# Graph layer on one core: PE results used two steps later, both sums of a two-tile batch together, fixed PSUM tiles, places turned in bfloat16

## The chip, the core and the metric

The kernel runs on one core of a Trainium2 chip. The core has TensorE (PE in the profile; PEld are its weight loads), VectorE (DVE), ScalarE (ACT), GpSimd (POOL) and SyncE (SP, which only issues DMAs here), each with an instruction stream of its own that runs in order; streams wait for each other through semaphores. The metric is the time of one execution in microseconds (us), the median of several runs.

## The reference

One layer of a graph network over 12,500 nodes of 64 features and 212,500 edges, which arrive sorted by one of their ends (`dst`), while the sums go by the other (`src`). Cut to what is computed:

```python
h = jnp.maximum(_layernorm(x, axis=-1), 0.0)
edge_in = jnp.concatenate([h[src], h[dst], edge_weight1], axis=1)
e = jax.nn.silu(edge_in @ eW1 + eb1)
e = jax.nn.silu(e @ eW2 + eb2)
agg = jax.ops.segment_sum(e, src, num_segments=h.shape[0])
node_in = jnp.concatenate([h, agg], axis=1)
out = x + jax.nn.silu(node_in @ nW1 + nb1) @ nW2 + nb2
```

## The kernel before

The nodes are dealt into NB = 100 buckets of L = 125. Two kinds of work run beside each other.

*Sending.* Edges come in 208 blocks of 1024. For each block `send` (line 439) forms the part of the first edge layer that depends on `dst` and the weight (`qp`, PE line 454), copies it to SBUF (`qs`, ACT lines 464 and 470, which also puts the place of the `src` node in its bucket beside it), and writes its rows to the table `q` in DRAM with eight indirect DMAs from POOL's queue (line 477). The row of each edge is its bucket and its rank there; `count` (line 375) finds the ranks on DVE (`oh`, `each`, `mine`, `rank`, `to`, lines 382 to 433) with PE's help (lines 396 and 414). A block is cut into three pieces.

*Steps.* The ranks are cut into twelve LEVELS; each names the tiles a batch takes (1 or 2) and the block by which its ranks are complete. A batch is one level of four buckets (G = 4), so that a level has 25 batches, and a step treats four 128-row tiles, a whole one-tile batch or half of a two-tile batch. There are 450 steps: two levels of one tile (steps 0 to 49), six of two tiles (50 to 349), four of one tile (350 to 449). Step k does, in functions of their own:

- `fetch` (519): SP loads the batch's rows `qt` from `q`, after its level's last scatter, and the buckets' `src` part `a`, unless it is kept in SBUF
- `s_lr` (560): four PE matmuls turn the places of the tiles across partitions (`lr`); `s_one_t` (569): DVE compares them with the partition number (`oneT`)
- `s_pt` (574): PE transposes the rows into `pt` and adds `a` times `oneT`; ACT takes the silu, `e1`
- `s_bias` (609): ACT writes the second bias into a PSUM tile; `s_p2` (615): PE adds `e1` times `w2` to it; ACT takes the silu, `e2`
- `s_one` (593): DVE compares places with node numbers (`one`); `s_seg` (625): PE sums `e2` by node into `seg`; `s_add` (634): DVE adds `seg` to `aggT` in SBUF

These are interleaved by hand: `manual_schedule` keeps PE, DVE, ACT and SP in program order, and `turn` says which step each function treats in turn k:

```python
turn = [
    (s_pt, 1), (s_add, -2), (s_one_t, 2), None, (s_bias, 1), (s_p2, 0), (s_one, 0), None, (s_seg, -1), None, (s_lr, 3), None,
]
```

A `None` is a place for other work: pieces of sending, spread evenly between `marks` so that a level's blocks are sent, with three blocks of lead (`LEAD`), some steps before its first; a feed of earlier stages; and, in the last level, pieces of the node layer. `nodes` (line 270) is a generator, one per batch: PE `z` from `aggT` (277), DVE adds the part of the features and ACT takes the silu (`zs`, 281 and 282), PE `o` (286), DVE adds the residual (`os`, 289). Up to two are advanced in alternate places.

PSUM has eight banks: a pool of four (`mm`) for `lr`, `pt`, `qp`, `z`, `o` and others in rotation, two for `p2`, one for `seg`, one for the counts. The fetched rows have NQ = 4 slots of two-tile size.

Of the kernel before, what the change touches and what calls it, by code (L numbers as in the profile page):

```python
# [62 lines left out]
FIRST_KEPT, LAST_KEPT = (0, 2, 5, 7, 10, 12, 15, 17, 20), 21  # L63
# [11 lines left out]
def tile_gnn(ctx: ExitStack, tc: tile.TileContext, x, src, dst, ew, eW1, eb1, eW2, eb2, nW1, nb1, nW2, nb2, out):  # L75
# [122 lines left out]
    def product(s, hr, ps, tag, to):  # L198

        abs_ = []  # L200
        for a in range(2):

            half = slice(a * D, (a + 1) * D)
            ab = ps.tile([P, G // 2, H], F32, name="ab", tag=tag)
            for i in range(G // 2):
                nc.tensor.matmul(ab[:, i], hr[half, i, :], w1[half, s, :], start=True, stop=True)  # L206
            abs_.append(ab)
        for a in range(2):
            nc.scalar.copy(to.rearrange("l (i a) h -> l a i h", a=2)[:, a], abs_[a])
# [34 lines left out]
    def node_part(B, ps, sb, tag):  # L244
# [6 lines left out]
        z = [ps.tile([P, G // 2, L], F32, name="zp", tag=tag) for _ in range(2)]  # L251
# [18 lines left out]
    def nodes(B, xr, zh, ps, sb, tag):  # L270
# [4 lines left out]
        z = [ps.tile([P, G // 2, L], F32, name="z", tag=tag) for _ in range(2)]  # L275
        for a in range(2):
            nc.tensor.matmul(z[a], w1g, aggT[:, b + a : b + G : 2, :], start=True, stop=True)
        send_out()
        yield
        for a in range(2):  # L280
            nc.vector.tensor_tensor(zs[:, a], z[a], zh[:, a], op=OP.add)
        nc.scalar.activation(zs, zs, AF.Silu, bias=nb1c)
        yield
        o = ps.tile([L, G, D], F32, name="o", tag=tag)
# [12 lines left out]
    qsp = ctx.enter_context(tc.tile_pool(name="qs", bufs=8))  # L297
    top = ctx.enter_context(tc.tile_pool(name="to", bufs=4))
    with ExitStack() as work:
        mm = work.enter_context(tc.tile_pool(name="mm", bufs=4, space=PSUM))  # L300
        p2p = work.enter_context(tc.tile_pool(name="p2", bufs=2, space=PSUM))
        sgp = work.enter_context(tc.tile_pool(name="sg", bufs=1, space=PSUM))
# [5 lines left out]
        full = sgp.tile([P, NB], F32, name="counts")  # L308
        nc.tensor.matmul(full, before, identb[:, :NB], start=True, stop=True)
        nc.vector.memset(full, -1.0)  # L310
        mine = cnt.tile([P, NB, TB], F32, name="mine")
        sums = []
# [61 lines left out]
        def count(s):  # L374

            if s < nblocks:
# [8 lines left out]
                each = wk.tile([P, NB], BF16, name="each")  # L385
# [53 lines left out]
        def send(s):  # L439
# [9 lines left out]
            qps = [mm.tile([P, 2, 2, H], F32, name="qp", tag="mm") for _ in range(2)]  # L449
# [8 lines left out]
            for i, qp in enumerate(qps):  # L458
# [7 lines left out]
            for i, same, qs in parts:  # L466
# [45 lines left out]
        steps = [(w, B, n, g) for w, B, n in batches for g in range(n)]  # L512
        PIECES = 1 + TB // G
# [3 lines left out]
        most = max(n for _, _, n in batches)  # L517

        def fetch(i):
            if i >= len(batches):  # L520
                return
            c, B, n = batches[i]
            assert not any(pending[: c + 1])
            while B not in done_a:
                next(feed)
            at = B * G * ROWS + G * (ENDS[c] - n * P)
            qt = ld2.tile([P, G * most, W], F32, name="qt")
            ins = nc.sync.dma_start(
                qt[:, : G * n, :].rearrange("p j w -> p (j w)"),
                q[at : at + G * n * P, :].rearrange("(p j) w -> p (j w)", p=P),  # L530
            ).ins
# [3 lines left out]
            tc.add_to_no_dep_group("loads", ins)  # L535
            if c == len(LEVELS) - 1 and not ndp:
# [3 lines left out]
                for name, bufs in (("nd_in", NQ + 5), ("nd", 2), ("al", NQ)):  # L540
                    ndp.append(work.enter_context(tc.tile_pool(name=name, bufs=bufs, side="right")))
            a = kept.get(B)
            if a is None:
# [4 lines left out]
                else:  # L548
                    a = ld2.tile([P, G, H], F32, name="a", bufs=NQ - 1)
                nc.sync.dma_start(a, ta_buckets[:, B * G : B * G + G])  # L550
            batch[c, B] = [qt, a, None]
            if c == len(LEVELS) - 1:
                node_in[B] = nodes_in(B, ndp[0])

        def of(k):

            c, B, n, g = steps[k]
            return batch[c, B], [((g * G + t) % n * G + (g * G + t) // n, (g * G + t) // n) for t in range(G)]

        def s_lr(k):  # L560
            (qt, _, _), tiles = of(k)
            loc = qt.rearrange("p j w -> p (j w)").bitcast(BF16)
            lr = mm.tile([P, G, P], F32, name="lr", tag="mm")
            for t, (j, _) in enumerate(tiles):
                at = 2 * (j * W + H) + 1
                nc.tensor.matmul(lr[:L, t, :], loc[:, at : at + 1].to_broadcast([P, L]), identb, start=True, stop=True)  # L566
            st[k] = {"lr": lr}

        def s_one_t(k):
            oneT = wk.tile([L, G, P], F32, name="oneT")  # L570
# [3 lines left out]
        def s_pt(k):  # L574

            (qt, a, _), tiles = of(k)
            oneT = st[k].pop("oneT")
            pt = mm.tile([P, G, P], F32, name="pt", tag="mm")
            for t, (j, _) in enumerate(tiles):
                nc.tensor.matmul(  # L580
                    pt[:, t, :], qt[:, j, :H], ident, is_transpose=True, start=t == 0, stop=False, skip_group_check=True
                )
            for b, same in itertools.groupby(range(G), lambda t: tiles[t][1]):
# [3 lines left out]
                    pt[:, cols, :], a[:L, b, :], oneT[:, cols, :], start=False, stop=True, skip_group_check=True  # L587
# [537 lines left out]
```

## Time and profile before

| | |
|---|---|
| runs | 2437.44, 2447.51, 2449.9 us; median 2447.51 |
| profiled execution | 2449.06 us, its span 2447.2 us |
| PE busy | 2047.0 us (84%), 16191 matmuls |
| DVE busy | 1882.0 us (77%) |
| POOL busy | 1723.1 us (70%), of it 1661 scatters 1691.0 us |
| ACT busy | 1101.4 us (45%) |
| granted PE clock, mean | 0.929 |

All times in the profile are from the start of the span. A line of a timeline has start, duration, engine, line of the program, operation, `out<-in` with shapes, and how many instructions of the kind were merged; in square brackets stands how long the engine had been idle before, and the instruction whose end released it. SPq and POOLq are the issuing queues. A line of waits has the engine and what waited, what it waited for, the total, the number of times and the longest one. The stretches' columns are named where they are shown.

### The profile page before, as it was taken

To read this page: it belongs to the slowest core of one execution; us is meant where nothing else is said; L and a number is where in the kernel's file an instruction comes from. 1 tells how busy PE (TensorE), PEld (TensorE's weight loads), DVE (VectorE), ACT (ScalarE), POOL (GpSimd) and SP (SyncE) were. 2 spreads that over 40 slices of the span, in tenths; PEclk is the share of its full clock that TensorE was granted. 3 is DMA by queue.
4 is the path that set the end of the run, shared out by engine and by line. 5 is a ranking of instruction groups with operands and counts; after the bars stand their busy time and mean duration, and the time that the engine had idled before them with its cause. 6 is when DMAs were issued, how large, how long until landed. Compare 5 with 4: busy or idle time off the path is not lost.

```text
span 2447.2 us, 45925 instructions
## 1 busy us (share of the span) xinstructions
PE 2047.0 (84%) x16191; PEld 1835.2 (75%) x16191; DVE 1882.0 (77%) x3058; ACT 1101.4 (45%) x2428; POOL 1723.1 (70%) x1712
## 2 busy tenths in 40 slices
PE   3673886655688898988989889999999999999998
PEld 2452665555677787877878778788888889899998
DVE  7985676666677787887878878888888888886665
ACT  2452443322344454444545444445555555555443
POOL 4677777777777777777777777777777777773210
PEclk9865898777799999999999999999999999999999
DMA  4564776555566654656644434444444444544674
GB/s 119 184 218 130 225 220 199 166 171 159 166 195 191 196 188 157 184 182 198 185 131 143 142 125 138 146 141 138 135 157 141 148 143 135 155 147 122 182 213 119
DMA packets 212956, 399.73 MB, mean 163 GB/s; under 512 B 47132, under 2 KB 112463, under 8 KB 212513
## 3 DMA queue, kind: packets, MB, share of 16 engines
q1 hardware_dynamic: 134581, 225.69, 30.8%
q0 software_dynamic: 53536, 123.03, 14.7%
q10 hardware_dynamic: 24602, 47.98, 6.8%
q8 instruction: 131, 2.15, 0.4%
q14 instruction: 106, 0.87, 0.1%
HBM read 200.58 MB, written 195.95 MB: 162 GB/s over the span
## 4 chain that ended last, share of the span: by engine, by line
PE 38%; DMA 19%; POOL 17%; DVE 14%; issue 9%; ACT 3%; SPq 0%; DVEq 0%; POOLq 0%; ACTq 0%
POOL q L477 17%; DMA q<-qs,to 16%; PE seg L632 9%; PE pt L586 8%; PE p L618 7%; PE qp L454 4%; PE pt L580 4%; PE lr L566 2%; DVE oneT L571 2%; DVE rank L431 2%; DVE each L387 1%; DVE one L599 1%; PE ab L206 1%; DVE mine L429 1%; DVE oh L382 1%
## 5 line engine op out<-in xcount | busy, mean ns | idle before, releaser
L477 POOL DMA_INDIRECT q<-qs,to x1661 | 1691.0, 1018 | 585.0 <-issue 393.2
L590 ACT ACTIVATE e<-pt 128x512 f32<-128x512 f32 x450 | 268.8, 597 | 822.3 <-PE pt L586 820.1
L632 PE MATMUL seg<-one,e 128*128 128x125 f32 x3600 | 499.1, 283 | 100.4 <-DVE aggT L643 59.3
L632 PEld LDWEIGHTS seg<-one,e 128*128 128x128 f32 x3600 | 451.5, 197 | 134.3 <-issue 74.3
L618 PEld LDWEIGHTS p<-w,e 128*128 128x128 f32 x3600 | 475.1, 197 | 46.5 <-issue 20.3
L618 PE MATMUL p<-w,e 128*128 128x128 f32 x3600 | 493.3, 281 | 0.0
L464 ACT COPY qs<-qp 128x512 f32<-128x512 f32 x416 | 224.7, 588 | 343.6 <-PE qp L454 292.5
L571 DVE TENSOR_SCALAR oneT<-lr,part 125x512 f32<-125x512 f32 x450 | 335.2, 745 | 52.5 <-PE lr L566 52.0
L431 DVE TENSOR_REDUCE rank<-mine 128x8 f32<-128x800 f32 x208 | 334.7, 1609 | 7.2
L599 DVE TENSOR_TENSOR one<-nodes,qt 128x500 f32<-128x500 f32 x450 | 301.8, 671 | 0.0
L454 PE MATMUL qp<-win,pick 64*128 64x256 f32 x1662 | 271.0, 438 | 35.2 <-DMA pick<-in_edge_weight_dram 15.2
L622 ACT ACTIVATE e<-p 128x512 f32<-128x512 f32 x450 | 269.1, 598 | 43.6 <-PE p L618 43.6
L580 PE MATMUL pt<-ident,qt 128*128 128x128 f32 x1800 | 286.7, 284 | 0.8 <-DVE oneT L571 0.8
L433 DVE SCALAR_TENSOR_TENSOR to<-rank,offE 128x8 int32<-128x8 f32 x208 | 36.5, 175 | 301.3 <-DMA q<-qs,to 296.4
L612 ACT COPY p<-b2f 128x512 f32<-128x512 f32 x450 | 267.2, 594 | 0.0
L643 DVE TENSOR_TENSOR aggT<-aggT,seg 128x500 f32<-128x500 f32 x275 | 184.1, 670 | 78.4 <-PE seg L632 78.1
L454 PEld LDWEIGHTS qp<-win,pick 64*128 64x128 f32 x1662 | 168.5, 206 | 101.1 <-issue 61.4
L586 PE MATMUL pt<-oneT,al 125*128 125x256 f32 (+1 forms) x1048 | 228.8, 351 | 13.4 <-DVE oneT L571 13.4
L580 PEld LDWEIGHTS pt<-ident,qt 128*128 128x128 f32 x1800 | 199.4, 147 | 43.7 <-issue 36.6
L429 DVE TENSOR_TENSOR mine<-oh,counts 128x800 f32<-128x800 bf16 x208 | 204.0, 981 | 19.2 <-PE counts L414 18.2
L387 DVE TENSOR_REDUCE each<-oh 128x100 bf16<-128x800 bf16 x208 | 205.1, 986 | 7.1
L566 PE MATMUL lr<-identb,qt 128*125 128x128 bf16 x1800 | 182.5, 225 | 24.3 <-DMA qt<-q 13.7
(156 smaller groups left out, 1847.0 us busy)
## 6 DMA issues: line engine op xcount, KB each, us to landing
qt<-q SPq DMA_DIRECT2D x150, 576.0 KB
qt<-q SPq DMA_DIRECT2D x150, 288.0 KB
q<-zeros ACTq DMA_DIRECT2D x25, 1080.0 KB
q<-qs,to POOLq DMA_INDIRECT x1661
q<-zeros ACTq DMA_DIRECT2D x10, 1440.0 KB
bc<-dests SPq DMA_DIRECT2D x103, 128.0 KB
win<-tb SPq DMA_DIRECT2D x416, 30.0 KB
a<-ta SPq DMA_DIRECT2D x45, 256.0 KB
```

The lines of the kernel that those rows point to most:

```text
L431: nc.vector.tensor_reduce(rank, mine.rearrange("p b t -> p t b"), AX.X, OP.add)
L454: nc.tensor.matmul(qps[i][:, t, : n_of[t]], pick[at, t * P : (t + 1) * P], win[at, : n_of[t]], start=True, stop=True)
L477: ins = nc.gpsimd.indirect_dma_start(out=q[:], out_offset=bass.IndirectOffsetOnAxis(ap=to[:k, j : j + 1], axis=0), in_=qs[:k, t, a, :], in ...
L571: nc.vector.tensor_scalar(oneT, st[k].pop("lr")[:L], part1[:L, :], None, op0=OP.is_equal)
L580: nc.tensor.matmul(pt[:, t, :], qt[:, j, :H], ident, is_transpose=True, start=t == 0, stop=False, skip_group_check=True)
L586: nc.tensor.matmul(pt[:, cols, :], a[:L, b, :], oneT[:, cols, :], start=False, stop=True, skip_group_check=True)
L590: nc.scalar.activation(e1, pt, AF.Silu)
L599: nc.vector.tensor_tensor(one.rearrange("p (b j) l -> p b j l", j=n), nodes1[:, None, None, :].to_broadcast(wide), loc[:, tiles[0][1] : ti ...
L612: nc.scalar.copy(p2, b2f)
L618: nc.tensor.matmul(p2[:, t, :], e1[:, t, :], w2, start=False, stop=t == G - 1, skip_group_check=True)
L622: nc.scalar.activation(e2, p2, AF.Silu)
L632: nc.tensor.matmul(item[2][:, b, :], e2[:, t, :], one[:, t, :], start=j < G, stop=j >= G * (n - 1))
```

## The change

- `turn` becomes one in which pt runs two steps ahead of p2 and seg two behind it (before: one and one); the load of a batch is issued six steps ahead, in slots for single steps (eight half slots), and `a` is loaded by a function of its own, four steps ahead; three `None` in place of four.
- `s_seg` treats both steps of a two-tile batch at the second of them.
- DVE's order in a turn becomes one, oneT, add (before: add, oneT, one); ACT's becomes e1, e2, bias (before: e1, bias, e2), with the bias written into the tile that e2 of two steps before has read.
- PSUM: eight tiles that live throughout, four of them handed out in rotation by `bank`; both halves of `z` share the bank of the counts, and one DVE addition takes them.
- `nodes` are advanced by `tick` at each `None`: z, zs, o and os of a batch at successive places, the next batch's z where the last one's os stands.
- `lr` is made by transposes with a bfloat16 result instead of matmuls with a float32 result.
- Fewer buckets' `a` are kept in SBUF: of the first pass 2, 8 and 15 (before: nine), then all up to 16 (before: 21).
- Halves are copied in reversed order in `product` and `send`; `each` has two fixed tiles; several pools get other numbers of buffers (`e1` 3, `one` and `e2` 4, from 2).

The core of the diff:

```diff
-FIRST_KEPT, LAST_KEPT = (0, 2, 5, 7, 10, 12, 15, 17, 20), 21
+FIRST_KEPT, LAST_KEPT = (2, 8, 15), 16
...
         zs = sb.tile([P, 2, G // 2, L], F32, name="zs", bufs=3)
-        z = [ps.tile([P, G // 2, L], F32, name="z", tag=tag) for _ in range(2)]
+        z = z_of()
         for a in range(2):
-            nc.tensor.matmul(z[a], w1g, aggT[:, b + a : b + G : 2, :], start=True, stop=True)
+            nc.tensor.matmul(z[:, a], w1g, aggT[:, b + a : b + G : 2, :], start=True, stop=True)
         send_out()
         yield
-        for a in range(2):
-            nc.vector.tensor_tensor(zs[:, a], z[a], zh[:, a], op=OP.add)
+        nc.vector.tensor_tensor(zs, z, zh, op=OP.add)
         nc.scalar.activation(zs, zs, AF.Silu, bias=nb1c)
         yield
-        o = ps.tile([L, G, D], F32, name="o", tag=tag)
+        o = o_of()
...
-        mm = work.enter_context(tc.tile_pool(name="mm", bufs=4, space=PSUM))
-        p2p = work.enter_context(tc.tile_pool(name="p2", bufs=2, space=PSUM))
-        sgp = work.enter_context(tc.tile_pool(name="sg", bufs=1, space=PSUM))
+        psum = work.enter_context(tc.tile_pool(name="psum", bufs=1, space=PSUM))
+        p2s = [psum.tile([P, G, H], F32, name=f"p2{i}") for i in range(2)]
+        seg = psum.tile([P, 4 * P], F32, name="seg")[:, : G * L].rearrange("p (b l) -> p b l", l=L)
+        free = itertools.cycle([psum.tile([P, 4 * P], F32, name=f"bank{i}") for i in range(4)])
...
-        def fetch(i):
-            if i >= len(batches):
+        def fetch(k):
+            if k in batch or k not in first_of:
                 return
...
+            i = k % (2 * NQ)
+            qt = qts[i // 2][:, i % 2 * G : (i % 2 + n) * G, :]
...
+            tc.declare_no_dep(ins, group="turned", reason="the comparison that read the places came after them")
...
+        def s_a(k):
+            c, B, n, g = steps[k]
+            if g == 0:
+                rows[c, B] = rows_of_a(c, B)
...
-            lr = mm.tile([P, G, P], F32, name="lr", tag="mm")
-            for t, (j, _) in enumerate(tiles):
-                at = 2 * (j * W + H) + 1
-                nc.tensor.matmul(lr[:L, t, :], loc[:, at : at + 1].to_broadcast([P, L]), identb, start=True, stop=True)
+            lr = bank(1, 2 * P)[:, 0].bitcast(BF16).rearrange("p (u e) -> p u e", u=G)
+            for u, (j, _) in enumerate(tiles):
+                loc = qt[:, j, H : H + 1].bitcast(BF16)[:, 1:2]
+                ins = nc.tensor.transpose(lr[:L, u, :], loc.to_broadcast([P, L]), identb).ins
...
-            p2 = p2p.tile([P, G, H], F32, name="p2")
-            nc.scalar.copy(p2, b2f)
-            st[k]["p2"] = p2
+            nc.scalar.copy(p2s[k % 2], b2f)
...
-            e2, one = st[k].pop("e2"), st[k].pop("one")
-            for t, (j, b) in enumerate(tiles):
-                nc.tensor.matmul(item[2][:, b, :], e2[:, t, :], one[:, t, :], start=j < G, stop=j >= G * (n - 1))
+            for i in range(k - n + 1, k + 1) if g == n - 1 else ():
+                e2, one = st[i].pop("e2"), st[i].pop("one")
+                for u, (j, b) in enumerate(of(i)[2]):
+                    nc.tensor.matmul(seg[:, b, :], e2[:, u, :], one[:, u, :], start=j < G, stop=j >= G * (n - 1))
...
+        def tick():
+
+            for t in list(going):
+                t[1] += 1
+                if next(t[0], 0) == 0:
+                    going.remove(t)
+            if tails and all(i > 2 for _, i in going):
+                B = tails.pop(0)
+                going.append([nodes(B, *node_in.pop(B), lambda: zb, lambda: bank(1, G, D)[:L, 0], ndp[1]), 1])
+                next(going[-1][0])
...
         turn = [
-            (s_pt, 1), (s_add, -2), (s_one_t, 2), None, (s_bias, 1), (s_p2, 0), (s_one, 0), None, (s_seg, -1), None, (s_lr, 3), None,
+            (s_pt, 2), (s_a, 4), (s_one, -1), (fetch, 6), (s_one_t, 3), (s_add, -3), None,
+            (s_p2, 0), (s_bias, 2), None, (s_seg, -2), None, (s_lr, 4),
         ]
...
-        first = -3
+        first = -4
...
-            start = w * (NB // G) - NQ
-            by = sum(x[2] for x in batches[: start + 1]) - 2
+            by = sum(n for _, _, n in batches[: w * (NB // G)]) - 6.5
...
-                    if tails:
-                        both = tails[at % 2 :: 2][:1] if len(tails) > 1 else tails[:1] * (at % 2)
-                        for t in both:
-                            if next(t, 0) == 0:
-                                tails.remove(t)
+                    tick()
```

More of the change, by code (lines that the diff above doesn't have):

```diff
@@ L250, in node_part @@
             yield
[L251 removed]
+        z = [bank(G // 2, L) for _ in range(2)]
         for a in range(2):
@@ L311, in tile_gnn @@
         mine = cnt.tile([P, NB, TB], F32, name="mine")
+        eachs = [cnt.tile([P, NB], BF16, name=f"each{i}") for i in range(2)]
         sums = []
```

154 lines of the change are left out of this document (79 added, 75 removed).

## The prediction

> **What bounds the kernel now.** I read the page first, then busy time by stretch, cut where one level of steps gives way to the next: steps 300-349 (two tiles a batch), then 350-374, 375-399, 400-424 and 425-449 (one tile a batch).
>
> ```profile
> span 2447.2 us, 45925 instructions
> ...
> 100.00:1835.00 1735.00, 1420.00 (x10792) 1248.11 (x10793) 1330.74 (x2125) 767.74 (x1736) 1334.17 (x1317) 0.91 0.54 170
> 1835.00:2030.00 195.00, 189.56 (x1569) 173.35 (x1568) 167.56 (x263) 104.05 (x223) 150.02 (x148) 1.00 0.45 143
> 2030.00:2128.00 98.00, 93.93 (x866) 88.67 (x866) 88.00 (x142) 50.20 (x106) 75.37 (x75) 1.00 0.50 149
> 2128.00:2222.00 94.00, 91.46 (x854) 87.97 (x854) 80.14 (x129) 48.78 (x102) 67.51 (x66) 1.00 0.50 149
> 2222.00:2310.00 88.00, 87.96 (x831) 86.30 (x830) 57.36 (x95) 43.84 (x87) 23.26 (x24) 1.00 0.46 133
> 2310.00:2447.00 137.00, 126.33 (x1080) 122.86 (x1078) 77.78 (x152) 56.05 (x98) 18.78 (x23) 0.99 0.60 175
> ```
>
> Columns: stretch, length, busy us and count of PE, PE loads, DVE, ACT and POOL, granted clock, DMA share, GB/s. POOL looks a quarter idle, but its own timeline says otherwise.
>
> ```profile
> 38.85 1.05 POOL L477 DMA_INDIRECT q<-qs,to  x1 [21.34 <-ACT qs L470]
> ...
> 2199.75 0.97 POOL L477 DMA_INDIRECT q<-qs,to  x1 [0.30 <-issue]
> 2201.03 0.97 POOL L477 DMA_INDIRECT q<-qs,to  x1 [0.30 <-issue]
> ...
> 2227.22 1.13 POOL L477 DMA_INDIRECT q<-qs,to  x1 [11.91 <-ACT qs L470]
> ...
> 2292.66 0.90 POOL L477 DMA_INDIRECT q<-qs,to  x1 [2.82 <-ACT qs L470]
> ```
>
> Each scatter holds POOL for 0.97 + 0.30 = 1.27 us, a block of eight for 10.2; in 100-1835, 1317 of them fill 1735 us. There POOL sets the pace, and what PE gains or loses is worth nothing. Beside steps 300-349 run 19 blocks (194 us of POOL in 195): balance. Beside 350-374 run ten (102 in 98), then eight, then three: POOL drops out (it first goes hungry before 2227), and PE is busy for 96-100%. From about 1835 on PE, with what it waits for, is the bound. Those waits of PE, nine rows from first to last, sum to 15.7 us:
>
> ```profile
> PE lr L566 <- DMA qt<-q: 4.8, 5, 1.1
> ...
> PE counts L414 <- DVE u L407: 0.4, 1, 0.4
> ```
>
> The last 25 steps also carry the node layer. One turn of that stretch, with the ACT and DVE work that matters:
>
> ```profile
> 2412.41 0.36 PEld L566 LDWEIGHTS <-qt 128*125 128x125 bf16 x4
> 2412.52 0.39 PE L566 MATMUL lr<-identb,qt 128*125 128x128 bf16 x4
> 2412.69 0.42 PEld L580 LDWEIGHTS pt<-ident,qt 128*128 128x128 f32 x4
> 2412.72 0.68 DVE L643 TENSOR_TENSOR aggT<-aggT,seg 128x500 f32<-128x500 f32 x1 [0.47 <-PE seg L632]
> 2413.09 0.97 PEld L586 LDWEIGHTS pt<-oneT,a_last 125*128 125x128 f32 x8
> 2413.32 0.74 DVE L571 TENSOR_SCALAR oneT<-lr,part 125x512 f32<-125x512 f32 x1
> 2413.98 0.73 PEld L277 LDWEIGHTS z<-aggT,w1g 128*128 128x128 f32 x4
> 2414.73 1.07 PEld L618 LDWEIGHTS p<-w,e 128*128 128x128 f32 x8
> 2414.78 0.59 ACT L612 COPY p<-b2f 128x512 f32<-128x512 f32 x1
> 2415.72 0.95 PEld L286 LDWEIGHTS o<-w2n,zs 128*125 128x125 f32 x8
> 2416.03 0.60 ACT L622 ACTIVATE e<-p 128x512 f32<-128x512 f32 x1 [0.65 <-PE p L618]
> 2416.52 0.70 ACT L282 ACTIVATE zs<-zs,nb1c 128x500 f32<-128x500 f32 x1
> 2416.59 0.97 PEld L632 LDWEIGHTS seg<-one,e 128*128 128x128 f32 x8
> 2417.48 0.36 PEld L566 LDWEIGHTS <-qt 128*125 128x125 bf16 x4
> ```
>
> A turn is 2417.48 - 2412.41 = 5.07 us, and PE never stops. It can do so because `o` at 2415.72 uses the `zs` of the turn before: this turn's is begun only at 2416.52.
>
> **The last stretch after the change.** The changed program's streams have, per turn: PE transposes, pt, z, p2, seg, o, lr; ACT e1, e2, bias, zs; DVE one, oneT, add, os, zs. Three things move: `add`, which `z` needs, comes behind `oneT`; `o` waits for the `zs` of its own turn; and the bias copy refills the PSUM tile that `e2` has just read, so it waits for `e2`, with `zs` queued behind both. What a handover costs is seen where PE stood still at the end:
>
> ```profile
> 2435.94 0.68 DVE L643 TENSOR_TENSOR aggT<-aggT,seg 128x500 f32<-128x500 f32 x1 [0.46 <-PE seg L632]
> 2436.67 0.72 PEld L277 LDWEIGHTS z<-aggT,w1g 128*128 128x128 f32 x4 [0.96 <-DVE aggT L643]
> ...
> 2438.34 0.71 ACT L282 ACTIVATE zs<-zs,nb1c 128x500 f32<-128x500 f32 x1 [3.00 <-DVE zs L281]
> 2439.10 0.95 PEld L286 LDWEIGHTS o<-w2n,zs 128*125 128x125 f32 x8 [0.63 <-ACT zs L282]
> 2440.28 0.42 DVE L289 TENSOR_TENSOR os<-o,xr 125x256 f32<-125x256 f32 x1 [1.16 <-PE o L286]
> ```
>
> 0.05 us each (2436.62 to 2436.67, 2439.05 to 2439.10). The new turn, counted from the issue of lr:
> - lr ends at 2412.52 + 0.39, so 0.50 after its issue; handover 0.05; oneT and add 0.74 + 0.68, less 0.08 overlap (add to oneT started 0.60 apart, add lasting 0.68), 1.34; handover 0.05. So z at 1.94, where PE alone would be there at 1.57: 0.37 lost.
> - z to p2 0.75 (2413.98 to 2414.73). p2's issue to e2 1.30 (to 2416.03). e2 0.60 + 0.05, then bias; zs 0.49 behind bias, as now behind e2; zs 0.70; handover 0.05: o comes 3.19 after p2. PE's own work between is p2 0.99 (to 2415.72) and seg 0.89 (2416.59 to 2417.48), 1.88: 1.31 lost.
> - o 0.87 (2415.72 to 2416.59). Sum 1.94 + 0.75 + 3.19 + 0.87 = 6.75 us, 1.68 more than now.
>
> Every link hangs on the one before it, round to the next lr, so nothing hides it. From the lr of step 430 to that of step 449 the present kernel makes 19 turns of 5.07, 96.3 us. The changed one starts z a turn later: one turn without (about 3.35) and 18 of 6.75, 124.9: +28.6. From there to the end it takes 2440.70 - 2417.48 = 23.2 us now. Changed: two more turns with bias (6.75, and 6.1 without lr), two without bias (0.75 + 1.30 + 0.49 + 0.70 + 0.05 + 0.87 = 4.2 each), three of z, seg and o at about 3.5 (z 1.1, DVE 0.7, ACT 0.7, o 0.9 and handovers), 0.7 for the last o and os: 32.3, +9.1. Together +37.7. If bias did not wait, 18 x 0.16 = 3 less; were each of the five handovers twice as dear, 5 more.
>
> **Steps 350-424.** There add falls due once a turn too:
>
> ```profile
> 2132.09 1.05 PE L632 MATMUL seg<-one,e 128*128 128x125 f32 x8
> 2134.44 0.67 DVE L643 TENSOR_TENSOR aggT<-aggT,seg 128x500 f32<-128x500 f32 x1
> 2135.02 0.74 DVE L571 TENSOR_SCALAR oneT<-lr,part 125x512 f32<-125x512 f32 x1
> 2135.44 1.05 PE L632 MATMUL seg<-one,e 128*128 128x125 f32 x8
> ```
>
> A turn is 3.35 us. Seg ended at 2133.14, DVE was busy with a block's ranks, add began 1.30 late and ended at 2135.11, just before the next seg. With oneT ahead of it (0.66) it ends at 2135.77, and seg waits some 0.4 us; queued behind seg are lr and so the next oneT. DVE is busy for 88 of 98 us here, so this recurs about once a block: 21 blocks x 0.4 = +8. Bounds: 0 (the qp group between two segs gives cover) and 0.5 in each of 50 turns, 25. For two-tile batches add has a turn more to spare, and both sums together cost PE what they cost apart: 0.
>
> **Smaller terms.** PE's 15.7 us of waits: the load now comes two turns ahead of lr instead of one, e1 and e2 two turns ahead of their use; I take -8, bounds 0 and -15.7. The other way, at step 350 the first load follows its level's last scatters two turns ahead of lr where it was four.
>
> ```profile
> SPq L528 <- DVE one L599: 1260.3, 274, 12.3
> ...
> SPq L528 <- DMA q<-qs,to: 19.0, 4, 12.3
> ...
> L391 DVE TENSOR_SCALAR pick<-bc,same,plus 128x512 f32<-128x512 bf16 x102 | 55.8, 547 | 0.0
> ```
>
> SP's queue stands 1260 us behind `one` today, with the edge weights' and windows' loads behind it; the load now takes a slot whose `one` is a turn old, so that wait goes, and since those loads cost PE next to nothing (the rows of its waits), so does the gain. SP has waited for scatters up to 12.3 us; two turns less of cover is 7.8; I take +3 (0 to 8), since three blocks are still sent ahead. Earlier levels: 0, under POOL. The places as bf16 transposes: same operands and count, so 0 for PE; at most what the float32 transposes take (0.40 against 0.28 a group, rows above) x 125 turns, +15. For oneT I keep 0.74: its output and its source memory stay; at best it gets as short as the 547 ns of `pick`, -0.2 x 18 = -4. (The Trainium skill, VectorE: DVE Perf Modes, "What auto-detection actually checks", asks 16 bits of every tensor for two elements a cycle out of PSUM; oneT writes float32, so by it the sum stays as it is.) Rows of `a` are loaded 104 times instead of 45 because fewer stay in SBUF; they come two turns ahead of pt, twice the lead that left `qt` 4.8 us of waits, so 0; without that cover, up to 1.1 us each for the 24 that fall into steps 350-424. Fixed slots in SBUF and PSUM and copies in reversed order issue nothing more: 0. Three places a turn for the scattered pieces instead of four: the same pieces, 0 under POOL, and in 350-424 the reason why I don't count on more cover for add than now.
>
> **Sum.** 2447.2 + 37.7 + 8 + 3 - 8 = 2487.9 us of span; outside it lie 2449.06 - 2447.2 = 1.9, and the profiled run is 1.6 above the median of 2447.51. So 2488, 1.7% slower.
>
> **Rivals.**
> - Faster, 2432: the two steps of slack do what they say, all 15.7 us of waits go, and the last turns stay at 5.07. Place: `o`, in the turn of its own zs. It decides at 1.88 us: if zs is there that soon after p2, PE does not stop. For: e2 to zs is 0.49 today. Against: e2 itself begins only 1.30 after p2, so 1.88 leaves no room for the bias copy and zs.
> - Only z's 0.37 is lost, o being covered by something I don't see: 2447.5 + 18 x 0.37 + 3 + 3 = 2460.
> - No change, 2447: POOL paces on to the end. Against: its 11.91 us of hunger before 2227, with PE at 100%.
> - Worse, 2525: add is late in every turn of 350-424 (25), the boundary costs 8, and transposes go at the float32 pace (15).
> - The clock: PE's granted share falls as lr becomes a transpose. Rows: 1.00 in 2222-2310, with four transposes among 831 / 25 = 33 matmuls a step; 0.91 in 100-1835, where PE waits on POOL. At 0.91 the 612 us from 1835 would last 60 longer: 2508 without the rest, 2548 with it. The Trainium skill (TensorE: Matmul & The Clock Gate, "Part 4: PE-mode transpose") says that transposes don't count as busy for the clock gate, which speaks for this rival; the 1.00 beside transposes speaks against it.
>
> **Chances and range.** Forecast 0.72 (its own range 2466 to 2512), faster 0.08, only z 0.08, no change 0.03, worse 0.07, clock 0.02. The range 2456 to 2512 takes in "only z" and leaves out both signs beyond. About 0.5% (12 us) is what a measurement can tell from no change: faster 0.08, same 0.06 (no change and part of "only z"), slower 0.86.
>
> **What would show it.** Right: in the changed profile PE idles before `o` for about 1.3 us, released by ACT zs, and before `z` for 0.4, released by DVE add, some 20 times each; turns of 6.7 us; PE busy falls well below 100% in the last 150 us. POOL's last scatter stays within 10 us of 2293. Wrong: turns near 5.1 with PE full, or the loss lying before the last scatter, or a granted clock under 0.98 in the end.

## The result and the profile after

The changed kernel takes 2480.88 us (median of four runs, 2478.09 to 2486.47) where the kernel before takes 2446.66 beside it: a ratio of 1.0149, with a 95% interval of 1.0116 to 1.0182. Predicted were 2488 us. The profiled execution spans 2478.8 us.

The same stretches as before, from the view of busy time by stretch of the changed kernel (stretch, length, busy us and count of PE, PE loads, DVE, ACT, POOL, then granted clock, DMA share, GB/s), and the end of POOL's timeline:

```profile
2030.00:2128.00 98.00, 89.03 (x789) 83.24 (x790) 84.07 (x137) 50.69 (x100) 75.15 (x76) 0.98 0.51 157
2128.00:2222.00 94.00, 90.34 (x832) 85.62 (x831) 75.88 (x124) 50.94 (x98) 62.65 (x61) 1.00 0.50 155
2222.00:2310.00 88.00, 86.19 (x812) 84.62 (x811) 55.27 (x90) 46.94 (x84) 19.25 (x19) 1.00 0.46 141
2310.00:2479.00 169.00, 135.17 (x1071) 123.96 (x1069) 74.11 (x128) 58.40 (x96) 18.76 (x25) 0.98 0.47 137
```

```profile
2289.73 0.90 POOL L485 DMA_INDIRECT q<-qs,to  x1 [6.02 <-ACT qs L478]
```

PE, which was busy for 92 to 100% of the stretches from 2030 on, is now busy for 91% of the first of them (96 before) and 80% of the last (92 before). POOL's last scatter comes at 2289.73 (2292.66 before), so POOL is not the reason. The granted clock is 0.98 in the first and the last of these stretches (1.00 and 0.99 before); 0.02 of 98 and of 169 us is 5 us at most (an estimate), and in the turns from 2320 to 2450 it is 1.00, so the clock is not the reason either. The three waits from 1835 on that the prediction turns on, before (line, releaser: us in total, times, longest):

```profile
PE z L277 <- DVE aggT L643: 2.4, 3, 0.9
PE seg L632 <- DVE aggT L643: 2.4, 3, 1.2
PE o L286 <- ACT zs L282: 0.5, 1, 0.5
```

After, the three longest of PE:

```profile
PE bank L284 <- ACT zs L280: 25.0, 25, 1.6
PE seg L647 <- DVE aggT L657: 12.5, 19, 2.6
PE bank L604 <- DVE oneT L588: 6.8, 6, 2.5
```

L284 is `o`: each of the 25 node layers makes PE stand for 1 us. The wait of `z` is not among them, since the modelled ends of the matmuls leave some 0.1 us of it; it shows in the weight loads, which come first (from 2311 on; `counts` is the bank in which `z` now lies):

```profile
PEld bank L284 <- ACT zs L280: 29.9, 25, 2.0
PEld counts L276 <- DVE aggT L657: 5.4, 19, 0.3
```

One turn of the last stretch, PE's weight loads (PEld) beside DVE and ACT:

```profile
2433.24 0.31 PEld L582 LDWEIGHTS <-qt 128*125 128x125 bf16 x4
...
2433.73 0.75 DVE L588 TENSOR_SCALAR oneT<-bank,part 125x512 f32<-125x512 bf16 x1 [2.89 <-PE bank L582]
...
2434.40 0.67 DVE L657 TENSOR_TENSOR aggT<-aggT,seg 128x500 f32<-128x500 f32 x1
...
2435.11 0.72 PEld L276 LDWEIGHTS counts<-aggT,w1g 128*128 128x128 f32 x4 [0.28 <-DVE aggT L657]
...
2435.86 1.07 PEld L635 LDWEIGHTS p<-w,e 128*128 128x128 f32 x8
...
2437.16 0.60 ACT L639 ACTIVATE e<-p 128x512 f32<-128x512 f32 x1 [1.50 <-PE p L635]
2437.79 0.59 ACT L630 COPY p<-b2f 128x512 f32<-128x512 f32 x1
2438.31 0.71 ACT L280 ACTIVATE zs<-zs,nb1c 128x500 f32<-128x500 f32 x1
...
2439.07 0.95 PEld L284 LDWEIGHTS bank<-w2n,zs 128*125 128x125 f32 x8 [1.25 <-ACT zs L280]
2439.94 0.31 PEld L582 LDWEIGHTS <-qt 128*125 128x125 bf16 x4
```

The turn is 2439.94 - 2433.24 = 6.70 us (5.07 before). The reader is to see the ring in it: oneT, then the sum, then z 0.28 us late; p2, then e2, bias, zs on ACT one behind the other, then `o` 1.25 us late (by its weight loads; 1.06 by its matmuls); and lr of the next turn only behind `o`.

Where the 31.6 us of span (2478.8 - 2447.2) arise is told by one operation that both traces record 450 times, the e2 of each step on ACT. Its start:

| e2 of step | before | after | after - before |
|---|---|---|---|
| 300 | 1829.5 | 1811.6 | -17.9 |
| 350 | 2028.3 | 2014.4 | -13.9 |
| 425 | 2311.8 | 2311.5 | -0.2 |
| 447 | 2421.1 | 2450.0 | +28.9 |
| end of the span | 2447.2 | 2478.8 | +31.6 |

So the changed kernel is ahead until step 350, gives that back by step 425, and loses some 32 in the turns with the node layer and what is left behind the last step (the drain).

### The profile page after: what moved, and what is told of

It is laid out like the page before. It is cut to its first block, busy times and chain, and to the rows that moved or that the text cites. A ratio compares the mean times of both kernels' runs of the same rounds, so it can differ in the third digit from the quotient of the medians.

```text
span 2478.8 us, 45692 instructions
## 1 busy us (share of the span) xinstructions
PE 2050.4 (83%) x16191; PEld 1829.4 (74%) x16191; DVE 1880.1 (76%) x3033; ACT 1173.8 (47%) x2427; POOL 1709.9 (69%) x1712
## 3 DMA queue, kind: packets, MB, share of 16 engines
q0 software_dynamic: 53536, 123.03, 14.5%
## 4 chain that ended last, share of the span: by engine, by line
PE 31%; DMA 20%; POOL 16%; DVE 13%; issue 9%; ACT 3%; SPq 1%; DVEq 0%; POOLq 0%; ACTq 0%
DMA q<-qs,to 19%; POOL q L485 16%; PE seg L647 7%; PE bank L604 7%; PE p L635 7%; PE bank L462 3%; PE bank L596 3%; DVE oneT L588 3%; DVE one L618 2%; PE bank L582 2%; DVE aggT L657 2%; DVE rank L439 1%; ACT e L639 1%; DVE oh L390 1%; DVE each L395 1%
## 5 line engine op out<-in xcount | busy, mean ns | idle before, releaser
L609 ACT ACTIVATE e<-bank 128x512 f32<-128x512 f32 x450 | 268.8, 597 | 779.5 <-PE bank L604 771.0
L588 DVE TENSOR_SCALAR oneT<-bank,part 125x512 f32<-125x512 bf16 x450 | 335.9, 746 | 154.7 <-PE bank L582 149.4
L472 ACT COPY qs<-bank 128x512 f32<-128x512 f32 x416 | 224.6, 586 | 205.5 <-PE bank L462 122.9
L596 PE MATMUL bank<-ident,qt 128*128 128x128 f32 x1800 | 284.2, 282 | 0.0
L462 PE MATMUL bank<-win,pick 64*128 64x256 f32 x1662 | 256.7, 425 | 21.6 <-DMA pick<-in_edge_weight_dram 8.3
L604 PE MATMUL bank<-oneT,al 125*128 125x256 f32 (+1 forms) x1104 | 242.0, 351 | 31.8 <-DVE oneT L588 31.8
L582 PEld LDWEIGHTS <-qt 128*125 128x125 bf16 x1800 | 165.0, 142 | 96.9 <-issue 90.8
L462 PEld LDWEIGHTS bank<-win,pick 64*128 64x128 f32 x1662 | 157.2, 198 | 89.4 <-issue 47.1
L422 PE MATMUL counts<-each,before 128*128 128x100 bf16 x208 | 44.8, 216 | 201.2 <-DVE each L395 168.7
L604 PEld LDWEIGHTS bank<-oneT,al 125*128 125x128 f32 x1104 | 174.2, 199 | 47.6 <-DVE oneT L588 37.9
```

The source lines that it names most:

```text
L462: nc.tensor.matmul(qps[i][:, t, : n_of[t]], pick[at, t * P : (t + 1) * P], win[at, : n_of[t]], start=True, stop=True)
L588: nc.vector.tensor_scalar(oneT, st[k].pop("lr")[:L], part1[:L, :], None, op0=OP.is_equal)
L596: ins = nc.tensor.matmul(pt[:, u, :], qt[:, j, :H], ident, is_transpose=True, start=u == 0, stop=False, skip_group_check=True,).ins
L604: nc.tensor.matmul(pt[:, cols, :], a[:L, b, :], oneT[:, cols, :], start=False, stop=True, skip_group_check=True,)
L609: nc.scalar.activation(e1, pt, AF.Silu)
```

## Experiments

Theory: the loss is the order of the last turns (`o` in the turn of its own zs, the bias copy ahead of zs, the sum behind oneT). Rivals: the loss comes from the fixed PSUM banks, from lr as transposes, or from the late sum alone.

The runs came in three groups. The first ran on chip 3 and the third on chip 8 (both marked B below): the granted clock over the profiled runs was 0.84 to 0.86, and the kernel before took 3090 and 3082 us there. The second ran on chip 2 with 0.92 to 0.93, as in the result, whose chip is not on record (both marked A). Totals of B are therefore not set against those of A; the last turns can be, since the clock is 1.00 there in both. The waits in the table are those of PE's weight loads in one such turn, "e2 425 to 449" is the time from the e2 of step 425 to that of step 449, and the ratio is to the kernel before that ran in the same group.

| kernel | clock | turn, us | `o` waits | z waits | e2 425 to 449 | ratio to before (95%) |
|---|---|---|---|---|---|---|
| before | A | 5.07 | 0 | 0 | 118.8 | 1 |
| after | A | 6.70 | 1.25 | 0.28 | 147.5 | 1.0149 (1.0116 to 1.0182) |
| after_again | A | 6.70 | 1.25 | 0.28 | 147.5 | 1.0155 (1.0138 to 1.0172) |
| own_turn | B | 5.69 | 0.58 | 0 | 134.4 | 1.0029 (0.9999 to 1.0059) |
| own_turn_2 | B | 5.69 | 0.58 | 0 | 133.0 | 1.0080 (1.0044 to 1.0116) |
| zs_first | B | 6.03 | 0.58 | 0.28 | 134.2 | 1.0104 (1.0041 to 1.0167) |
| o_next_turn | B | 5.42 | 0 | 0.28 | 123.4 | 1.0109 (1.0047 to 1.0171) |
| add_first | B | 6.34 | 1.25 | 0 | 140.3 | 1.0142 (1.0072 to 1.0211) |
| add_first_2 | B | 6.34 | 1.25 | 0 | 140.3 | 1.0157 (1.0089 to 1.0226) |
| orders_alone | A | 6.77 | 1.16 | 0.43 | 157.1 | 1.0194 (1.0177 to 1.0211) |
| lr_matmul | A | 6.70 | 1.25 | 0.28 | 147.5 | 1.0160 (1.0143 to 1.0177) |
| both | A | 5.07 | 0 | 0 | 115.3 | 0.9920 (0.9904 to 0.9937) |
| old_marks | B | 6.70 | 1.25 | 0.28 | 147.5 | 1.0204 (1.0135 to 1.0273) |
| both_lead2 | B | 5.07 | 0 | 0 | 115.3 | 1.0020 (0.9991 to 1.0049) |

**own_turn.** The kernel before, its node layers stepped as in the changed one:

```diff
-                    if tails:
-                        both = tails[at % 2 :: 2][:1] if len(tails) > 1 else tails[:1] * (at % 2)
-                        for t in both:
-                            if next(t, 0) == 0:
-                                tails.remove(t)
+                    for t in list(tails):
+                        if next(t, 0) == 0:
+                            tails.remove(t)
```

> This is the kernel before with one thing changed: a node layer takes its next part at every place of a turn, so that `o` comes behind seg and uses the zs of its own turn, as in the changed kernel; the order of ACT (bias ahead of e2), the sums and the loads stay as before. Theory (the loss of the changed kernel is the cycle p2, e2, zs, o): `o` can start 1.30 + 0.49 + 0.70 + 0.05 = 2.54 us after p2, PE's own work between is 1.88, so PE stands 0.66 us before `o` in each turn, the turn of the last stretch goes from 5.07 to 5.73, and 18 turns and the drain cost 12 to 16 us: about 2462 against 2447. Rival (own turn alone is harmless; the changed kernel loses by the bias copy and the late add only): turn 5.07 to 5.2, 2447 to 2450.

Its timeline in the last stretch:

```profile
2990.13 1.07 PEld L618 LDWEIGHTS p<-w,e 128*128 128x128 f32 x8
...
2991.43 0.60 ACT L622 ACTIVATE e<-p 128x512 f32<-128x512 f32 x1 [0.65 <-PE p L618]
2991.93 0.70 ACT L282 ACTIVATE zs<-zs,nb1c 128x500 f32<-128x500 f32 x1
2992.68 0.95 PEld L286 LDWEIGHTS o<-w2n,zs 128*125 128x125 f32 x8 [0.58 <-ACT zs L282]
```

From p2 to `o` it takes 2992.68 - 2990.13 = 2.55 us (expected 2.54), and the turn is 5.69 (expected 5.73). Own turn alone makes PE stand, and the rival falls. The stretch from step 425 to 449 costs 14 to 16 us more than in the kernel before. The total tells little. own_turn_2 was the same kernel again, for its total: 13 to 16 us more were expected. Against the kernel before beside them, the two runs are 7 and 29 us longer, and the intervals of both ratios take in 14 to 16 us.

**zs_first.** The changed kernel, bias behind zs:

```diff
-            (s_p2, 0), (s_bias, 2), None, (s_seg, -2), None, (s_lr, 4),
+            (s_p2, 0), None, (s_bias, 2), (s_seg, -2), None, (s_lr, 4),
```

> The changed kernel with the bias copy of a turn put behind zs on ACT; nothing else differs. Theory: zs no longer stands behind the bias copy; it started 0.52 us after bias and would now start there where bias did, so the wait before `o` falls from 1.25 to about 0.7 us, the turn from 6.70 to about 6.15, and the time by 18 x 0.55 and some of the drain, 10 to 13 us: about 2469. Rival (the refill by bias is not on the cycle, because what `o` waits for is the DVE sum ahead of zs): turn stays at 6.70, 2481.

```profile
3039.14 0.60 ACT L639 ACTIVATE e<-p 128x512 f32<-128x512 f32 x1 [1.50 <-PE p L635]
3039.64 0.70 ACT L280 ACTIVATE zs<-zs,nb1c 128x500 f32<-128x500 f32 x1
3040.24 0.59 ACT L630 COPY p<-b2f 128x512 f32<-128x512 f32 x1
3040.39 0.95 PEld L284 LDWEIGHTS bank<-w2n,zs 128*125 128x125 f32 x8 [0.58 <-ACT zs L280]
```

The wait before `o` falls from 1.25 to 0.58 us and the turn to 6.03; steps 425 to 449 take 13.3 us less. In the changed kernel bias began 0.63 us behind e2 and zs 0.52 behind bias; now zs begins 0.50 behind e2, 0.65 sooner. So the bias copy is 0.67 us of the ring (1.25 - 0.58). The rival, a turn of 6.70, falls.

**o_next_turn.** Two empty steps, so that `o` comes between p2 and seg of the next turn:

```diff
         nc.scalar.activation(zs, zs, AF.Silu, bias=nb1c)
+        yield
+        yield
         yield
         o = o_of()
```

> The changed kernel with `o` of a node layer one turn later, between p2 and seg of the next turn, so that two layers are under way; z and zs stay where they are. Theory: the cycle through zs is open; what is left is PE's own 5.07 us and the wait of z for the sum behind oneT (0.28), a turn of 5.35, so 18 x 1.35 = 24 us less, and 0 to 9 less in the drain: 2448 to 2457. Rival (the loss sits in the late sum and the last turns are bound by DVE or ACT): the turn stays above 6, 2470 or more.

```profile
3014.67 1.07 PEld L637 LDWEIGHTS p<-w,e 128*128 128x128 f32 x8
3015.66 0.95 PEld L286 LDWEIGHTS bank<-w2n,zs 128*125 128x125 f32 x8
...
3019.34 0.72 PEld L276 LDWEIGHTS counts<-aggT,w1g 128*128 128x128 f32 x4 [0.28 <-DVE aggT L659]
```

`o` follows p2 without a wait, z still waits 0.28, and the turn is 5.42 (expected 5.35). Steps 425 to 449 take 24.1 us less (expected 24). The largest part of the loss is this one place.

**add_first and add_first_2.** The sum ahead of one and oneT on DVE:

```diff
-            (s_pt, 2), (s_a, 4), (s_one, -1), (fetch, 6), (s_one_t, 3), (s_add, -3), None,
+            (s_pt, 2), (s_a, 4), (s_add, -3), (s_one, -1), (fetch, 6), (s_one_t, 3), None,
```

> The changed kernel with the sum (add) ahead of one and oneT in DVE's order of a turn; nothing else differs. Theory: z no longer waits for the sum (0.28 us x 18 turns = 5 us, since z lies in the same cycle as `o`), and the waits of seg for the sum in steps 350 to 424 go (12.5 us, and the turns of 4.05 us where 3.35 is usual, 14 of them, become usual ones): 13 to 19 us less, 2462 to 2468; the time from the e2 of step 350 to that of step 425 falls from 297 to about 284. Rival (the waits of seg stand for a DVE that is full there, and the time only moves to pt, which then waits for oneT): 0 to 6 us less, pt waiting for oneT by as much as seg did for the sum.

> The changed kernel with the sum (add) ahead of one and oneT, run again because the first run fell on the chip with the clock of 0.85, where only the last turns could be read (6.36 us instead of 6.70). Theory for a clock near 0.93: 14 us less in steps 350 to 424, 18 x 0.33 = 6 in the last turns, and before step 350 the 14 us by which the version with both edits was ahead there, since the other edit touches the last 25 steps only: 32 to 35 less than the changed kernel, 2443 to 2447. Rival (the 14 us before step 350 have another source, a run's own scatter): 18 to 21 less, 2458 to 2461.

```profile
3017.20 0.68 DVE L657 TENSOR_TENSOR aggT<-aggT,seg 128x500 f32<-128x500 f32 x1 [1.10 <-PE seg L647]
...
3020.60 0.73 PEld L276 LDWEIGHTS counts<-aggT,w1g 128*128 128x128 f32 x4
```

The sum now starts as soon as seg is done, z waits for nothing, and the turn falls by 0.36 us to 6.34 (by 0.28 expected). What it is worth in steps 350 to 424 and before could not be read in B (350 to 424 takes 361 us there, with PE's own pauses); it is read below, in A.

**orders_alone.** The kernel before with own_turn's stepping and the changed orders of add and bias, and nothing else of the change:

```diff
-            (s_pt, 1), (s_add, -2), (s_one_t, 2), None, (s_bias, 1), (s_p2, 0), (s_one, 0), None, (s_seg, -1), None, (s_lr, 3), None,
+            (s_pt, 1), (s_one_t, 2), (s_add, -2), None, (s_p2, 0), (s_bias, 1), (s_one, 0), None, (s_seg, -1), None, (s_lr, 3), None,
```

> The kernel before with nothing of the change but three places in its orders: the sum (add) behind oneT on DVE, the bias copy behind e2 on ACT, and a node layer's next part at every place of a turn, so that `o` uses the zs of its own turn. PSUM, loads, lr, the steps of slack and the rest stay as before. Theory (the loss is these orders and nothing else): the last turns go from 5.07 to 6.65 to 6.75 us, 18 x 1.65 = 30 us and 2 to 6 in the drain, and in steps 350 to 424 a late sum in some turns, 5 to 14: 37 to 50 us more than the kernel before, so more than the changed kernel, which has other gains. Rival (part of the loss comes from the fixed PSUM banks or from the transposes): the turn stays below 6.4 and the cost below 25 us.

It takes 2486.51 us, 46 more than the kernel before beside it (37 to 50 were expected). PE's longest waits from 1835 on:

```profile
PE o L286 <- ACT zs L282: 23.6, 25, 1.3
PE seg L632 <- DVE aggT L643: 14.2, 23, 1.5
PE z L277 <- DVE aggT L643: 9.2, 23, 1.2
```

These are the same two waits as in the changed kernel, and the same late sum before seg. Three places in the orders are enough for the whole loss and more; the PSUM banks, the transposes, the loads and the second step of slack are not needed for it. Why its turn of 6.77 is a little longer than the changed kernel's (z waits 0.43 us, not 0.28) was not looked into.

**lr_matmul.** The changed kernel, lr by matmul into float32:

```diff
-            lr = bank(1, 2 * P)[:, 0].bitcast(BF16).rearrange("p (u e) -> p u e", u=G)
+            lr = bank(G, P)
...
-                ins = nc.tensor.transpose(lr[:L, u, :], loc.to_broadcast([P, L]), identb).ins
+                ins = nc.tensor.matmul(lr[:L, u, :], loc.to_broadcast([P, L]), identb, start=True, stop=True).ins
```

> The changed kernel with lr again by matmuls into a float32 bank, as in the kernel before, and oneT reading float32; the places are the same numbers. Theory: four matmuls of 128x128 took as long as four transposes (0.39 us a group in both kernels) and oneT 0.74 in both, so the time is that of the changed kernel, within 4 us. Rival (a transpose gives PE's clock less credit, or moves its two-byte results slower): 15 us less or more, and a granted clock that differs by 0.01 or more.

It takes 2478.15 us, the unaltered changed kernel beside it 2478.57. oneT in the groups of the changed kernel, and of this one:

```profile
L588 DVE TENSOR_SCALAR oneT<-bank,part 125x512 f32<-125x512 bf16 x450 | 335.9, 746 | 154.7 <-PE bank L582 149.4 <-issue 3.1 <-ACT e L639 1.5
```

```profile
L588 DVE TENSOR_SCALAR oneT<-bank,part 125x512 f32<-125x512 f32 x450 | 335.6, 746 | 154.0 <-PE bank L582 146.9 <-issue 3.9 <-ACT e L639 1.5
```

746 ns from either type, and lr's matmuls average 227 ns in both kernels. bfloat16 places change nothing here. The mean granted clock of the two profiled runs, 0.921 with matmuls and 0.932 with transposes, differs by as much as the rival asked for, but over all four runs of each kernel it is 0.921 to 0.931 with matmuls and 0.920 to 0.932 with transposes: that is one range, and the times agree within 0.4 us. The rival by which transposes lower the clock has nothing for it. (That rival went with the Trainium skill, TensorE: Matmul & The Clock Gate, "Part 4: PE-mode transpose", which says that transposes do not count as PE-busy in the same way; here, where lr makes four of some 33 matmuls a step and the four that turn the rows are transposes in both kernels, the runs show no such effect.)

**after_again and both.** The changed kernel unaltered, and with the later `o` and the earlier sum together.

> The changed kernel unaltered, as the measure for the others of this call, since the four earlier experiments ran on a chip with a granted clock of 0.85 where the first two runs had 0.93. Theory: whatever the clock of the earlier steps, the last turns are 6.70 us (clock 0.98 to 1.00 there). With a granted clock near 0.93 the time is 2475 to 2490, with 0.85 it is 3115 to 3140.

> The changed kernel with two of the edits already looked at together: the sum (add) ahead of one and oneT on DVE, and `o` one turn later. Theory: with both waits of the last turns gone the turn is PE's own, 5.05 to 5.15 us (5.42 with the later `o` alone, of which the wait of z for the sum is 0.3); the waits of seg in steps 350 to 424 go as well. Against the changed kernel of this call 18 x 1.6 = 29 us in the last turns, 0 to 6 in the drain, 10 to 14 in steps 350 to 424: 39 to 49 us less; on a chip with a clock near 0.93 that is 2432 to 2442, 5 to 15 us below the kernel before. Rival (DVE is full once the sum comes first, and pt waits for oneT instead): turn 5.3 or more, no gain over the kernel before.

after_again repeats the result: 2478.57 us. `both` takes 2419.99 us, 59 less than that (39 to 49 were expected) and 0.8% less than the kernel before (ratio 0.9920, 0.9904 to 0.9937). One turn of it:

```profile
2344.58 0.36 PEld L584 LDWEIGHTS <-qt 128*125 128x125 bf16 x4
...
2346.14 0.73 PEld L276 LDWEIGHTS counts<-aggT,w1g 128*128 128x128 f32 x4
...
2347.88 0.95 PEld L286 LDWEIGHTS bank<-w2n,zs 128*125 128x125 f32 x8
...
2349.34 0.71 ACT L280 ACTIVATE zs<-zs,nb1c 128x500 f32<-128x500 f32 x1
2349.65 0.36 PEld L584 LDWEIGHTS <-qt 128*125 128x125 bf16 x4
```

The turn is 5.07 us, and PE has no wait in it: `o` at 2347.88 uses the zs of the turn before, and this turn's begins at 2349.34. By the e2 of each step, `both` gains on the changed kernel 14.7 us up to step 350, 14.5 from 350 to 425 (282.6 us against 297.1; the kernel before has 283.4) and 32.3 from 425 to 447, and gives back 0.9 in the drain. The middle one confirms that the late sum was what the changed kernel lost in steps 350 to 424; the first was not expected by the theory for single edits and is taken up below.

**old_marks.** The changed kernel with the blocks' due time of the kernel before:

```diff
-            by = sum(n for _, _, n in batches[: w * (NB // G)]) - 6.5
+            by = sum(n for _, _, n in batches[: w * (NB // G)]) - 8
```

> The changed kernel with one number back: a level's blocks must be sent out 8 turns ahead of its first step, as in the kernel before, where the change has 6.5; all else as changed. At the e2 of step 300 the changed kernel is 17.9 us ahead of the kernel before, at block 176 of the scatters 10.9: so about 7 us ahead against its own blocks. Theory: these 7 come from the 1.5 turns (of 3.9 to 4.7 us, so 6 to 7): step 300 comes 6 to 7 us later and the time is 2484 to 2487 where the changed kernel has 2478.6. Rival (all of it comes from scatters that hold POOL for 1005 ns instead of 1015): no change, 2476 to 2481.

(In the kernel before it was 8 turns for the levels that begin at steps 100 to 350, and 5 for the others.) The time says nothing, since the run fell into B. The place of the steps against the blocks does: at the e2 of step 300 the `to` of block 172 is still 9.5 us off in the kernel before, 17.6 in the changed one, 17.6 to 18.2 in the others of A that are made from it, and 11.3 with the old due time (20.5 on the same chip without it, in add_first_2). So the 1.5 turns do move the steps ahead, by 8 to 9 us; whether the end moves with them stays open.

**both_lead2.** `both` with the blocks sent two ahead of need:

```diff
-        LEAD = 3 * PIECES
+        LEAD = 2 * PIECES
```

> The faster version (sum first and `o` a turn later) with the blocks sent two ahead of need instead of three, so that each level's steps begin a block (10.4 us of POOL) earlier against the scatters. Theory: what PE does before POOL drops out comes off the end, so up to 10 us less, 2410 to 2414. Rival: the load that opens a level then reaches SP's queue before the level's last scatters are done (SP already waits up to 12.2 us for scatters), the loads queued behind it come late and POOL runs dry: 2420 to 2440, with waits of POOL for ACT qs and of SP for scatters above 100 us in all.

The steps do run further ahead (32.8 us before block 172, where `both` had 18.2 in A). The time is the same as the kernel before's in B (1.0020, 0.9991 to 1.0049); POOL waited 752 us for ACT qs, but own_turn, which is not altered there, waited 708, so that mark tells nothing in B. The run is inconclusive.

The changed kernel with as many rows of `a` kept in SBUF as before was not tried, so what the added loads cost by themselves stays open.

## Why the prediction was right

**Last turns: right, in size too.** Predicted 6.75 us a turn, measured 6.70. Counted as the prediction counts, from issue to issue, 1.31 was to be lost between p2 and `o`, and 3.21 - 1.88 = 1.33 is; between lr and z 0.37 was to be lost, and (2435.11 - 2433.24) - 1.57 = 0.30 is. (The idle times of 1.25 and 0.28 in the rows are a little shorter.) From the lr of step 430 to that of 449 the changed kernel takes 124.0 us (predicted 124.9) and the kernel before 96.5. From there to the end of the last os it takes 2472.12 + 0.42 - 2439.94 = 32.6 (predicted 32.3; 23.2 before). Each of the three causes named there was shown by an edit of its own: own turn (own_turn), bias (zs_first), sum behind oneT (add_first), and together they reproduce the loss in the old kernel (orders_alone).

**Steps 350-424: mechanism right, size too small.** The wait of seg for the late sum is there (12.5 us), and falls to 2.6 us when the sum comes first (`both`). It was put at +8; the steps take 297.1 us instead of 283.4, +13.7, within the bounds of 0 to 25. It comes about as often as the "once a block" that I took (19 waits, 21 blocks), but a wait lasts 12.5 / 19 = 0.66 us on average, and up to 2.6, where I took 0.4.

**Before step 350: wrong.** "There POOL sets the pace, and what PE gains or loses is worth nothing" left out that the pace itself can change. The changed kernel is 13.9 us ahead at step 350. The scatters hold POOL for less (POOL's groups from 260 to 1835 us: kernel before, after, `both`):

```profile
L477 POOL DMA_INDIRECT q<-qs,to x1195 | 1212.8, 1015 | 363.9 <-issue 285.1 <-DMA q<-qs,to 35.6 <-ACT qs L470 6.1
```

```profile
L485 POOL DMA_INDIRECT q<-qs,to x1202 | 1208.4, 1005 | 367.9 <-issue 282.1 <-DMA q<-qs,to 40.4 <-ACT e L639 7.9
```

```profile
L487 POOL DMA_INDIRECT q<-qs,to x1211 | 1206.5, 996 | 369.9 <-issue 294.3 <-DMA q<-qs,to 37.2 <-DVE to L443 5.5
```

10 ns less for some 1200 scatters is 12 us, 19 ns is 23 us; at block 176 the changed kernel is 10.8 us ahead of the kernel before and `both` 23.5. In these traces that accounts for most of the lead; part of it is the earlier due time of the steps (old_marks), which is down to 2.3 us by step 349. What makes the scatters shorter stays open, and so does how much of it is the change's: the scatters of one kernel differ from run to run as well (1003 and 995 ns in the two runs of own_turn, in B; 1005 and 1007 in after and after_again, in A), and the one trace of the kernel before in A is of a run of 2449.06 us, near the top of its range there (2433.7 to 2449.9). orders_alone, with the loads, slack and PSUM tiles of the kernel before, is 11.5 us ahead at step 350 too (1005 ns), so those are not needed for the lead.

**PE's waits, -8: not so.** The load's waits (4.8 us) are gone, but from 1835 to 2030 pt now waits 6.8 us for oneT, and PE's waits there are 7.4 us where they were 5.3. The level boundary (+3) shows no wait of lr at step 350: 0.

**The start of the last stretch.** I measured it from lr, and counted the turn more by which lr runs ahead of the end only in the drain. In the changed kernel lr stands a turn earlier against e2, which makes the lr of step 430 come 5.0 us earlier than before where e2 of step 425 comes 0.2 earlier. So the sum is -13.9 + 13.7 - 4.8 + 27.4 + 9.4 - 0.2 (behind the last os) = 31.6, against the predicted -8 + 8 + 3 + 28.6 + 9.1 = 40.7. The terms of the last turns, 28.6 and 9.1, were off by 1 us together, the others by 8, and that is what the forecast of the span was too high by. The last turns were foreseen by their mechanism. That the rest came out within 8 us is partly luck: a lead of 13.9 that was not foreseen stands against a loss in steps 350 to 424 that was 5.7 larger than foreseen.

**SP's wait on DVE one: wrong, and worth nothing, as said.** It was to go; the changed kernel still has it, as the view of SP's waits shows:

```profile
SPq L535 <- DVE one L618: 962.0, 221, 10.8
```

**Rivals.** "Faster" failed at the point named for it: 1.88 us from p2 to `o` was the limit, and 3.21 is what it takes (2435.86 to 2439.07). Its premise, that the rest of the change helps, was right: with the waits of the last turns taken out, `both` is below the 2432 that this rival had. "Only z" (2460), "no change" and "worse" fall with the turn of 6.70. The rival of the clock falls with 1.00 in the last turns.

## What to carry to other kernels

When a stage is spread over turns, draw the ring of one turn (which instruction waits for which, and what stands ahead of it in its own queue) and set it against the work of the engine that bounds the turn: one wait of 1.25 us, met in each of the last turns, cost 24 of the 32 us (by o_next_turn). A deeper pipeline elsewhere does not help a ring that closes within a turn; `o` moved on by a turn and a sum moved forward in its queue turned +1.5% into -0.8%. Where another engine sets the pace, ask also what makes that engine's own instructions longer or shorter.

## What was not expected of the hardware

**A scatter takes longer beside some DVE instructions.** From the timelines of the kernel before, DVE and POOL:

```profile
1406.26 0.66 DVE L599 TENSOR_TENSOR one<-nodes,qt 128x500 f32<-128x500 f32 x1
```

```profile
1405.14 0.97 POOL L477 DMA_INDIRECT q<-qs,to  x1 [0.30 <-issue]
1406.42 1.34 POOL L477 DMA_INDIRECT q<-qs,to  x1 [0.30 <-ACT qs L470]
1408.07 0.97 POOL L477 DMA_INDIRECT q<-qs,to  x1 [0.31 <-issue]
```

Of the 604 scatters that begin between 1000 and 1800 us, 101 are longer than 1.05 us. Sorted by the DVE instruction that ran when they began (the later one where two overlap), they are 65 of the 82 beside `one` (mean of the 82: 1.24), 19 of 44 beside `oh` and 17 of 24 beside `pick`; of the 112 beside `rank`, the 41 beside `mine` and the 100 beside `oneT`, none (mean 0.97). In the changed kernel it is 62 of 88 for `one`, in `both` 63 of 81. `one` and `oh` are float32 and bfloat16 comparisons of two tiles in SBUF; `mine` and the sum have one of their two in PSUM; `pick` reads one tile, in bfloat16, with a number for each partition. The Trainium skill (SBUF — State Buffer, "Who interferes with whom") says that a DVE instruction with two SBUF inputs contends with a GpSimd instruction that reads SBUF, and infers that it does not hold up the writing of descriptors; the counts for `one`, `oh`, `rank` and `mine` agree with the first, and those for `one` speak against the second, for these indirect scatters. Fewer scatters are long after the change (101 of 604 before, 80 of 609 after, 68 of 611 in `both`), which fits the shorter means above. The scatters beside `one` are about as many; those beside `oh` fall from 44 to 23 and 13. No run changed that alone, so it is not shown to be the cause.

**One kernel, 26% apart between A and B.** In own_turn (B) the clock is 0.89 in a stretch in which PE is busy for 79% and 1.00 in one with 97% (same columns as above):

```profile
1200.00:1835.00 635.00, 502.37 (x3476) 433.47 (x3475) 406.71 (x644) 235.98 (x512) 378.69 (x379) 0.89 0.40 127
...
2900.00:2970.00 70.00, 67.69 (x608) 65.42 (x607) 39.66 (x71) 32.03 (x61) 12.88 (x15) 1.00 0.61 190
```

POOL, which hardly waits in A, waits in B for ACT qs, which copies what PE forms for a block (waits of POOL in the kernel before in A, then in own_turn in B):

```profile
POOL q L477 <- ACT qs L470: 84.4, 37, 21.3
```

```profile
POOL q L477 <- ACT qs L470: 707.8, 167, 21.4
```

So POOL does not set the pace of the first 350 steps in B as it does in A, and what an edit there is worth cannot be carried from one to the other; the last turns are the same to 0.02 us (6.70 in after_again and old_marks, 5.07 in `both` and both_lead2). What makes PE pause in B, and whether it lies with chips 3 and 8 themselves, is open.
